# The sums of an attention group turned and inverted by one instruction each

## Chip, cores and metric

The kernel runs on one core of a Trainium2 chip. The metric is device time in microseconds (us) of one execution. Before the change three runs took 3507.87, 3508.98 and 3513.93 us, so the median is 3508.98.

## What is computed

One transformer block with adaptive layer norm: eight sequences of 1024 tokens, 512 features, 16 heads, everything in float32. A condition vector per sequence gives six modulation rows. They scale and shift two layer norms and gate the two residual additions, one of causal attention and one of an MLP with GELU.

```python
mod = jax.nn.silu(condition) @ Wada + bada
sh_a, sc_a, gt_a, sh_m, sc_m, gt_m = jnp.split(mod, 6, axis=1)
xm = layernorm(x, g1, be1) * (1.0 + sc_a[:, None, :]) + sh_a[:, None, :]
q, k, v = split_heads(xm @ Wqkv)                      # 16 heads of 32
scores = jnp.where(causal, q @ k.T * 32 ** -0.5, -jnp.inf)
attn = jax.nn.softmax(scores, axis=-1) @ v
x = x + gt_a[:, None, :] * (attn @ Wproj + bproj)
xm = layernorm(x, g2, be2) * (1.0 + sc_m[:, None, :]) + sh_m[:, None, :]
h = jax.nn.gelu(xm @ W1 + b1, approximate=False)
return x + gt_m[:, None, :] * (h @ W2 + b2)
```

## The kernel before

**Tiles and stages.** The tokens are cut into 16 blocks of 512 (`n` from 0 to 15; two for each sequence, an even one and an odd one, and the odd one also attends to the keys of the even one). The 16 heads of a block are cut into four groups of four (`g` from 0 to 3), because four heads of 32 features fill the 128 partitions. So there are 64 groups `(n, g)`.

**Attention of a group.** TensorE computes score tiles of four heads (`sc`, L1679) into `st`, one tile of four PSUM banks that scores and weights share. VectorE adds the causal mask on diagonal parts (L1691) and reduces each tile to row maxima (`mx`, L1694). In a few places scores are made one head at a time in the three other PSUM banks instead (`scores_by_heads`, L1649 and L1666), which is allowed when none of these is in use. The maxima are split into three bf16 parts (L1713 to L1716) and turned into a row by TensorE (L1732, copied by ScalarE at L1738). Then the scores are computed again transposed, with the maxima subtracted by a matmul (L1758, L1770), ScalarE takes the exponential (L1782) into one of three `pT` tiles, GpSimd clears what the mask excludes (L1787), TensorE multiplies by the values into `po` (L1810), and GpSimd adds the `pT` tiles of the group up (L1911).

**End of a group.** `finish` multiplies the added weights by a column of ones, which gives the softmax sums of four heads in a bank: 128 partitions by 512 tokens, where the 32 partitions of one head all hold the same 512 sums. ScalarE copies the bank to `rec` (L1840) and `po` to `top` (L1843). Only 4 x 512 of the 128 x 512 values are different, so not all are inverted. VectorE's transpose turns each 32 x 32 block on its own. After it, each column of a block is a copy of one column of 32 sums, so one column of each block is enough. `gather(i)` does this for a quarter of the tokens: it turns 128 columns of `rec` into the small tile `squares` (L1850) and inverts 4 of them (every 32nd) into `inverse` (L1852). `spread_out` turns `inverse`, read with each column repeated 32 times, back into `rec` (L1857), and `quotient` multiplies `top` by `rec` into `qT` (L1885, on GpSimd in most groups). `rec`, `top`, `squares` and `inverse` have one buffer each. For most groups the four `gather` and the `quotient` are put on a list of jobs. The group `first_end` and the last group do them at once, and the last group works on its four quarters one after the other.

**Linear work.** Between the attention instructions TensorE runs the projections, the MLP and the modulation (L217; L524 for the gates `a` and `m`), whose products go through the same three PSUM banks and are taken out by VectorE (L208, L194) or ScalarE (L197, L204). Weights come through a ring of eight buffers, loaded on SP's queue (L362, L364, L366). Early in the run sums of weight quarters are prepared for later use: `prep_up` and `prep_down` are loaded (L854), added on VectorE or GpSimd (L167, L170) and stored to DRAM as `kept_up_S` and `kept_down_S` (L823). Every DMA but a few is issued by SP, in order. Most blocks have their normalized rows turned by way of DRAM: `held_a` is stored (L713) and read back into `hat_a` (L718), and then scaled and shifted into `xm_a` (L775 on VectorE, L781 on ScalarE). The first two and the last two blocks have theirs turned by TensorE (L771).

**What sets the order.** The kernel writes each engine's order out by hand, with a planner. While it is being built, it keeps a clock for each engine (`now`) and a due time for each piece of data. Each `note(engine, ns, reads, writes)` moves these on by a planned cost. By them it decides at each step whether TensorE goes on with attention or with linear work (`step_aside`, `work`), whether a copy goes to VectorE or ScalarE (`sooner`), whether an addition goes to VectorE or GpSimd (`either`), and when a job is let in: `run_jobs` takes the next job once the planned VectorE clock and the job's data are not later than TensorE's.

```python
while jobs and (
    everything or (now["DVE"] <= now["PE"] and due(jobs[0][1]) <= now["PE"])
):
    jobs.pop(0)[0]()
```

The planned cost of a piece is 160 + 1.05 x 128 + 100 = 394 ns, that of a spread of 512 columns 140 + 1.05 x 512 = 678 ns. `norm_columns` (L486 to L496) runs twice, once for each layer norm; its intermediate `one_plus` has one buffer.

Of the kernel before, what the change touches and what calls it, by code (L numbers as in the profile page):

```python
# [9 lines left out]
F32 = mybir.dt.float32  # L10
# [12 lines left out]
def kernel(  # L23
# [33 lines left out]
    nc = tc.nc  # L57
    B, T, D = x.shape
    HD = W1.shape[1]
    P = 128  # L60
    hd = D // H
    scale = float(hd) ** -0.5
    TB = 512
    NTT = TB // P
    NHALF = T // TB
    NC = D // P
# [15 lines left out]
    small = ctx.enter_context(tc.tile_pool(name="small", bufs=2))  # L82
# [22 lines left out]
    def due(reads=(), writes=()):  # L105
        t = 0.0
        for k in reads:
            t = max(t, written.get(k, 0.0))
        for k in writes:
            t = max(t, left.get(k, 0.0))  # L110
        return t

    def note(engine, ns, reads=(), writes=(), port=False):
        start = max(now[engine], due(reads, writes))
        if port:
            start = max([start] + [b for a, b in pool_spans if a <= start < b])
        end = start + ns
        now[engine] = end
        if engine == "POOL":
            pool_spans.append((start, end))  # L120
            del pool_spans[:-16]
        for k in reads:
            left[k] = max(left.get(k, 0.0), end + SYNC)
        for k in writes:
            written[k] = end + SYNC
        return end
# [9 lines left out]
    def note_pe(ns, form, reads=(), writes=()):  # L136
        now["PE"] = max(now["PE"], due(reads, writes))
        if shape[0] != form:
            shape[0] = form
            now["PE"] += SWITCH  # L140
        note("PE", ns, reads)
        spent[0] += ns
        for k in writes:
            written[k] = now["PE"] + PIPE

    def note_act(ns, func, reads=(), writes=()):
        if func is not None and table[0] != func:
            table[0] = func
            ns += TABLE
        note("ACT", ns, reads, writes)  # L150
# [31 lines left out]
    def lin_bank():  # L182
        i = min(
            (i for i in range(3) if not live[i]),
            key=lambda i: left.get(("l", i), 0.0),
        )
        live[i] = True
        return i
# [54 lines left out]
    def mlp_steps(n):  # L243
        return [("u", n, i) for i in range(NQ)] + [("d", n, part) for part in range(4)]
# [9 lines left out]
    for w in range(1, NB):  # L254
        n = w - 1
        m = mlp_steps(n)
# [29 lines left out]
    n = NB - 1  # L286
# [115 lines left out]
    Q = P // NTT  # L402
# [81 lines left out]
    def spread(o):  # L484
        return cols[:, o : o + NC].unsqueeze(2).to_broadcast([P, NC, B])

    def norm_columns(name, shift_at, gain_at, o_g, o_b):

        gain = const.tile([P, NC, B], F32, tag=f"gain{name}", name=f"gain{name}")
        shift = const.tile([P, NC, B], F32, tag=f"shift{name}", name=f"shift{name}")  # L490
        one_plus = small.tile([P, NC, B], F32, tag="onep", name=f"onep{name}", bufs=1)
        nc.vector.tensor_scalar(one_plus, modT[:, ts(gain_at, NC), :], 1.0, None, ALU.add)
        nc.vector.tensor_tensor(gain, one_plus, spread(o_g), ALU.mult)
        nc.vector.tensor_tensor(shift, one_plus, spread(o_b), ALU.mult)
        nc.vector.tensor_tensor(shift, shift, modT[:, ts(shift_at, NC), :], ALU.add)
        return gain, shift  # L496
# [60 lines left out]
    def add_job(job, reads, first=False):  # L557

        at = sum(1 for other in jobs if other[2]) if first else len(jobs)
        jobs.insert(at, (job, reads, first))  # L560

    def run_jobs(everything=False):
# [4 lines that stand above are left out]
# [854 lines left out]
    def perform(step):  # L1421
        kind = step[0]
        if kind == "mod":
            yield from modulation(step[1])
        elif kind == "norm_columns_a":
            columns_of["a"] = norm_columns("a", 0, 1, O_G1, O_BE1)
        elif kind == "gates":
            yield from gates(step[1])
# [112 lines left out]
    def step_aside(reads, writes):  # L1541


        while threads():
            if linear_wait() == NEVER:
                hurry()
            own, other = wait_of((reads, writes)), linear_wait()
            if done_linear[0] < stream["due"]:
                if other > own + 100:
                    break  # L1550
            elif own <= max(other, 50):
                break
            work()
        while BANK in writes and bank_at() == NEVER:
            work()
        run_jobs()
        run_act_jobs()
        run_pool_jobs()
        run_preparation()
# [260 lines left out]
    def finish(n, g):  # L1820

        run_jobs(True)
        acc, slot = totals.pop((n, g))
        more = unadded if (n, g) == first_end else []
        step_aside([("acc", n, g), *(("p", slot) for *_, slot in more)], [BANK])
        bank = lin_bank()
        terms = [(0, TB, acc, slot)] + [(c0, w, pT, slot) for parts, pT, slot in more for _, c0, w, _ in parts]
        for i, (c0, w, term, held) in enumerate(terms):
            for j in range(HPG):
                r = slice(j * hd, (j + 1) * hd)  # L1830
                nc.tensor.matmul(  # L1831
                    banks[bank][r, TB - w :], ones, term[:, j, c0 : c0 + w],
                    start=i == 0, stop=i == len(terms) - 1, skip_group_check=True,
                )
            note_pe(2 * COLUMN * w, "columns", [("acc", n, g), ("p", held)], [("l", bank)])
        free_p.extend([slot, *(held for *_, held in more)])
        top = tmp.tile([P, TB], F32, tag="top", name=f"top_{n}_{g}", bufs=1)
        rec = tmp.tile([P, TB], F32, tag="rec", name=f"rec_{n}_{g}", bufs=1)
        kr = "rec"
        nc.scalar.copy(rec, banks[bank])  # L1840
        note_act(585, None, [("l", bank)], [kr])
        live[bank] = False
        nc.scalar.copy(top, outs.pop((n, g)))  # L1843
        note_act(585, None, ["po"], ["top"])
        part = TB // 4
        wide = TB // 4

        def gather(i):
            squares = small.tile([P, wide], F32, tag="squares", name=f"squares_{n}_{g}_{i}", bufs=1)
            nc.vector.transpose(squares, rec[:, ts(i, wide)])  # L1850
            some = inverse[:, ts(i, wide // Q)]
            nc.vector.reciprocal(some, squares.rearrange("p (a i) -> p a i", i=Q)[:, :, 0])  # L1852
            note("DVE", 160 + 1.05 * wide + 100, [kr], [kr])

        def spread_out(i=0, m=TB):
            some = inverse[:, i * m // Q : (i + 1) * m // Q].unsqueeze(2).to_broadcast([P, m // Q, Q])
            nc.vector.transpose(rec[:, ts(i, m)].rearrange("p (a i) -> p a i", i=Q), some)  # L1857
            note("DVE", 140 + 1.05 * m, [kr], [kr])

        inverse = small.tile([P, TB // Q], F32, tag="inverse", name=f"inverse_{n}_{g}", bufs=1)  # L1860
        if (n, g) == groups[-1]:
            for i in range(NTT):
                gather(i)
                spread_out(i, part)
                some = slice(i * part, (i + 1) * part)
                nc.vector.tensor_tensor(qTs[n][:, g, some], top[:, some], rec[:, some], ALU.mult)
                note("DVE", 200, [kr, "top"], [("att", n, i)])
            return

        if (n, g) == first_end:  # L1870
            for i in range(4):
                gather(i)
            spread_out()
            nc.vector.tensor_tensor(qTs[n][:, g, :], top, rec, ALU.mult)
            note("DVE", 700, [kr, "top"], [("att", n)], port=True)
            written["attended", n] = 0.0
            return

        def quotient():
            spread_out()  # L1880
            if n == NB - 1 and g == NC - 2:
                nc.vector.tensor_tensor(qTs[n][:, g, :], top, rec, ALU.mult)
                note("DVE", 700, [kr, "top"], [("att", n)], port=True)
            else:
                nc.gpsimd.tensor_tensor(qTs[n][:, g, :], top, rec, ALU.mult)  # L1885
                note("POOL", 1285, [kr, "top"], [("att", n)])
            if g == NC - 1:
                written["attended", n] = 0.0

        for i in range(4):  # L1890
            add_job(lambda i=i: gather(i), [kr], g == NC - 1)
        add_job(quotient, [kr], g == NC - 1)

    shared = {}
# [194 lines left out]
```

## Time and profile before

| | |
|---|---|
| median of three runs | 3508.98 us |
| the profiled execution, its own time | 3501.11 us |
| its span, first to last instruction | 3499.4 us |
| mean granted clock of TensorE | 0.998 |
| bytes moved by DMA | 498.84 MB, 143 GB/s on average |

The profile shows one execution. Busy time of an engine is the time in which it executes; register and semaphore instructions don't count. Groups of instructions are named by line, engine, operation and tiles (out<-in, with the shapes of both), and then come the count, the busy time in us, the mean ns of one, the idle time of the engine just before them, and what ended that idle time. A float32 matmul of the program shows as two records. A wait is named as engine, tile and line, "<-", what released it: total us, times, longest. A row of the timeline gives start and length in us, engine, line, operation, tiles and shapes, the number of instructions merged, and in brackets the idle time before with its releaser. The granted clock is a share of full speed.

### The profile page before, as it was taken

How to read it: one execution, taken by the hardware profiler on the slowest of the kernel's cores; microseconds unless marked ns; L12 is line 12 of the kernel's file. 1: busy time of each engine (PE TensorE's matmuls, PEld its weight loads, DVE VectorE, ACT ScalarE, POOL GpSimd, SP SyncE). 2: the span in 40 equal slices, each digit the busy share in tenths (PEclk: the TensorE clock that was granted, in tenths of full speed). 3: DMA queues.
4: the chain of work that ended last, by engine and by line, in shares of the span. 5: the costliest groups of instructions: out<-in, count | busy, mean ns of one | idle time of the engine just before them, and what ended most of it. 6: DMA issues, size and time to landing. Idle time of an engine off the chain costs nothing. (4 is left out here: it accounts for less than half of the span.)

```text
span 3499.4 us, 122173 instructions
## 1 busy us (share of the span) xinstructions
PE 3441.3 (98%) x55101; PEld 1750.9 (50%) x55101; DVE 2203.8 (63%) x2808; ACT 1212.8 (35%) x1272; POOL 2113.7 (60%) x2255
## 2 busy tenths in 40 slices
PE   8999999999999999999999999999999999999999
PEld 4444455445544555445554455544555445554555
DVE  5775675565666566565666656665666656656573
ACT  2335333342343513335232442333423333323521
POOL 3667847667366663767627676375762857628640
PEclk9999999999999999999999999999999999999999
DMA  6763444535535455363554535545455454543344
GB/s 213 237 188 104 137 125 139 147 104 171 147 118 158 119 162 149 103 182 116 152 152 127 159 116 152 153 137 146 130 154 143 130 144 132 154 126 98 104 134 140
DMA packets 335580, 498.84 MB, mean 143 GB/s; under 512 B 27724, under 2 KB 184460, under 8 KB 331476
## 3 DMA queue, kind: packets, MB, share of 16 engines
q1 hardware_dynamic: 334944, 490.99, 47.8%
q8 instruction: 434, 7.11, 0.8%
q14 instruction: 86, 0.70, 0.1%
q10 hardware_dynamic: 116, 0.03, 0.0%
HBM read 432.13 MB, written 56.69 MB: 140 GB/s over the span
## 5 line engine op out<-in xcount | busy, mean ns | idle before, releaser
L1911 POOL TENSOR_TENSOR pT<-pT,pT 128x256 f32<-128x256 f32 (+3 forms) x1254 | 1224.7, 1012 | 238.9 <-PE po L1810 123.9
L1782 ACT ACTIVATE pT<-st 128x2048 f32<-128x2048 f32 x288 | 541.1, 1879 | 1017.5 <-PE st L1770 886.3
L217 PE MATMUL bank<-w,hT 128*32 128x256 f32 x14336 | 822.1, 380 | 0.0
L1694 DVE TENSOR_REDUCE mx<-sc 128x4 f32<-128x2048 f32 (+3 forms) x383 | 663.3, 1753 | 200.5 <-PE sc L1679 194.7
L217 PEld LDWEIGHTS bank<-w,hT 128*32 128x32 f32 x14336 | 448.0, 110 | 389.8 <-issue 109.7
L217 PE MATMUL bank<-xm_m,w 128*32 128x256 f32 x8192 | 497.4, 381 | 2.3 <-ACT p_u L197 1.0
L217 PE MATMUL bank<-t_m,w 128*32 128x256 f32 x6144 | 384.0, 380 | 2.5 <-DVE qT L208 1.4
L217 PEld LDWEIGHTS bank<-xm_m,w 128*32 128x32 f32 x8192 | 255.5, 110 | 227.3 <-issue 56.6
L1787 POOL TENSOR_SCALAR_AFFINE_SELECT pT<-pT 128x512 f32<-128x512 f32 x256 | 177.3, 710 | 313.7 <-ACT pT L1782 313.3
L1679 PE MATMUL sc<-kT,qT 32*128 32x512 f32 (+3 forms) x3064 | 328.0, 520 | 3.1 <-DVE mx L1694 1.8
L1691 DVE TENSOR_TENSOR sc<-sc,mask 128x1024 f32<-128x1024 f32 (+1 forms) x160 | 162.8, 1017 | 255.2 <-PE sc L1679 210.8
L1810 PE MATMUL po<-pT,v 128*32 128x512 f32 (+3 forms) x3048 | 301.7, 490 | 2.5 <-POOL pT L1787 2.3
L1770 PE MATMUL st<-qT,kT 32*128 32x512 f32 (+3 forms) x3072 | 302.7, 487 | 0.0
L217 PEld LDWEIGHTS bank<-t_m,w 128*32 128x32 f32 x6144 | 188.9, 110 | 178.8 <-issue 49.8
L217 PE MATMUL bank<-xm_a,w 128*32 128x256 f32 x3968 | 241.6, 380 | 2.4 <-ACT p_k L197 1.1
L1679 PEld LDWEIGHTS sc<-kT,qT 32*128 32x128 f32 x3064 | 129.2, 183 | 182.4 <-issue 82.4
L208 DVE TENSOR_TENSOR hT<-bank,u_u 128x512 f32<-128x512 f32 x186 | 126.0, 686 | 127.2 <-PE bank L217 126.5
L217 PE MATMUL bank<-t_a,w 128*32 128x256 f32 x2944 | 182.3, 380 | 1.4 <-ACT qT L204 0.9
L1885 POOL TENSOR_TENSOR qT<-top,rec 128x512 f32<-128x512 f32 x61 | 79.8, 1309 | 170.7 <-DVE rec L1857 167.8
L217 PE MATMUL bank<-w,qT 128*32 128x512 f32 (+1 forms) x1824 | 175.4, 515 | 3.7 <-DMA w<-in_L_cond_Wproj_dram 3.7
L1199 ACT ACTIVATE hT<-hT,cols 128x512 f32<-128x512 f32 x256 | 164.7, 711 | 40.7 <-DVE hT L208 27.4
L217 PEld LDWEIGHTS bank<-xm_a,w 128*32 128x32 f32 x3968 | 123.9, 110 | 101.3 <-issue 16.9
(262 smaller groups left out, 3657.1 us busy)
## 6 DMA issues: line engine op xcount, KB each, us to landing
w<-in_L_cond_W_dram SPq DMA_DIRECT2D x384, 256.0 KB
w<-kept_up_S SPq DMA_DIRECT2D x256, 256.0 KB
w<-kept_down_S SPq DMA_DIRECT2D x256, 256.0 KB
w<-kept_qkv_S SPq DMA_DIRECT2D x180, 256.0 KB
w<-in_L_cond_Wqkv_dram SPq DMA_DIRECT2D x147, 256.0 KB
hat_a<-in_x_dram SPq DMA_DIRECT2D x64, 256.0 KB
xr<-in_x_dram SPq DMA_DIRECT2D x32, 512.0 KB
out_dram<-xr SPq DMA_DIRECT2D x31, 512.0 KB
```

What stands on the lines that cost most here:

```text
L208: nc.vector.tensor_tensor(out, src, other, op)
L217: nc.tensor.matmul(ps[r, :], columns, rhs, start=start, stop=stop, skip_group_check=True)
L1199: nc.scalar.activation(hT[:, i, :], hT[:, i, :], AF.Gelu, bias=cols[:, O_B1 + f : O_B1 + f + 1])
L1679: nc.tensor.matmul(sc[:, j, c0 : c0 + w], qTs[n][r, gg, ts(qt, P)], keys_of(n, kh)[r, gg, :w], start=True, stop=True, skip_group_check=True,)
L1691: nc.vector.tensor_tensor(place, place, shape_of.to_broadcast(place.shape), ALU.add)
L1694: nc.vector.tensor_reduce(maxima[n, gg][:, kh, qt, :], sc[:, :, c0 : c0 + w], axis=AX.X, op=ALU.max)
L1770: nc.tensor.matmul(st[:, j, c0 : c0 + w], kT[r, gg, ts(k % NTT, P)], qT[r, gg, TB - w :], start=False, stop=True, skip_group_check=True,)
L1782: nc.scalar.activation(pT[:, :, :used], st[:, :, :used], AF.Exp, scale=scale)
L1787: nc.gpsimd.affine_select(diagonal, diagonal, pattern=[[0, HPG], [1, P]], compare_op=ALU.is_ge, fill=0.0, base=0, channel_multiplier=-1,)
L1810: nc.tensor.matmul(po[r, TB - w :], v[:, k % NTT, g * P + j * hd : g * P + (j + 1) * hd], pT[:, j, c0 : c0 + w], start=(k == 0), stop=last ...
L1885: nc.gpsimd.tensor_tensor(qTs[n][:, g, :], top, rec, ALU.mult)
L1911: nc.gpsimd.tensor_tensor(into, into, pT[:, j, c0 : c0 + w], ALU.add)
```

## The change

`gather` no longer uses `squares`. It turns a whole stretch of `rec` in place, 512 columns for most groups, and inverts every 32nd column of it, 16 in one instruction. So a group has one job for it where it had four. The last group still goes by quarters of 128 columns, in place too. The planned costs are written anew: 325 + 1.27 x 512 = 975 ns for the whole gather, where the four pieces had 4 x 394 = 1578 ns, and 180 + 1.04 x 512 = 712 ns for the spread. `one_plus` gets two buffers, its pool's default. Lines behind L1846 move up by two to four: the turn is at L1848, the reciprocal at L1850, the spread at L1855 and the product at L1882.

```diff
-        one_plus = small.tile([P, NC, B], F32, tag="onep", name=f"onep{name}", bufs=1)
+        one_plus = small.tile([P, NC, B], F32, tag="onep", name=f"onep{name}")
...
-        wide = TB // 4
-
-        def gather(i):
-            squares = small.tile([P, wide], F32, tag="squares", name=f"squares_{n}_{g}_{i}", bufs=1)
-            nc.vector.transpose(squares, rec[:, ts(i, wide)])
-            some = inverse[:, ts(i, wide // Q)]
-            nc.vector.reciprocal(some, squares.rearrange("p (a i) -> p a i", i=Q)[:, :, 0])
-            note("DVE", 160 + 1.05 * wide + 100, [kr], [kr])
+
+        def gather(i, m=TB):
+            nc.vector.transpose(rec[:, ts(i, m)], rec[:, ts(i, m)])
+            some = inverse[:, i * m // Q : (i + 1) * m // Q]
+            nc.vector.reciprocal(some, rec[:, ts(i, m)].rearrange("p (a i) -> p a i", i=Q)[:, :, 0])
+            note("DVE", 325 + 1.27 * m, [kr], [kr])
 
         def spread_out(i=0, m=TB):
...
-            note("DVE", 140 + 1.05 * m, [kr], [kr])
+            note("DVE", 180 + 1.04 * m, [kr], [kr])
...
         if (n, g) == groups[-1]:
             for i in range(NTT):
-                gather(i)
+                gather(i, part)
                 spread_out(i, part)
...
         if (n, g) == first_end:
-            for i in range(4):
-                gather(i)
+            gather(0)
             spread_out()
...
-        for i in range(4):
-            add_job(lambda i=i: gather(i), [kr], g == NC - 1)
+        add_job(lambda: gather(0), [kr], g == NC - 1)
         add_job(quotient, [kr], g == NC - 1)
```

## The prediction

> **What bounds the kernel now.** I read the busy times first, then the run cut into stages, then TensorE's waits by stage, then the groups that the diff touches.
>
> ```profile
> span 3499.4 us, 122173 instructions
> PE 3441.3 (98%) x55101; PEld 1750.9 (50%) x55101; DVE 2203.8 (63%) x2808; ACT 1212.8 (35%) x1272; POOL 2113.7 (60%) x2255
> 0.00:118.00 118.00, 102.07 (x1877) 59.18 (x1877) 75.65 (x113) 32.94 (x40) 52.66 (x74) 1.00 0.69 221
> 118.00:477.00 359.00, 348.50 (x5304) 168.02 (x5304) 248.81 (x318) 130.13 (x127) 262.34 (x290) 0.99 0.51 156
> 477.00:3300.00 2823.00, 2798.86 (x44716) 1417.89 (x44708) 1772.95 (x2231) 996.14 (x1043) 1729.95 (x1834) 1.00 0.48 138
> 3300.00:3499.40 199.40, 191.88 (x3221) 105.78 (x3212) 106.36 (x147) 53.63 (x64) 68.74 (x59) 0.99 0.44 131
> ```
>
> In a stage row stand its bounds, its length, the busy time of PE, PEld, DVE, ACT and POOL, the granted clock, DMA's share and GB/s. PE is busy for 3441.3 of 3499.4 us, so all waits together are 58.1 us: 15.9 in the first stage, 10.5 in the second, 24.1 in the third, 7.5 in the last. The matmuls are the same before and after, so a gain can only come out of these waits (and out of stretches at a lower clock). VectorE, which the change relieves, is idle for 37% of the span.
>
> I cut at 118 and 477 us because of the change's second effect. The kernel records its instructions in an order that it plans with the costs in `note`. I compared both programs' orders on TensorE, counting four column-tile matmuls as one step: the first 425 steps are the same; then, up to the weights of block 2, group 2 (`st_2_2_2`, the 44th exponential, at 478.96 us here), only 1477 of 1726 stand in the same sequence; of the 9994 after that, 9901 do, from block 3 to the end. So the change is a reordering in the second stage and nearly nothing but shorter DVE work in the third.
>
> **The gather.** The last number before the second bar is the mean ns of one instruction; in the row of L686 stand minimum, median and maximum; in the two timeline rows start and length in us.
>
> ```profile
> L1850 DVE STREAM_TRANSPOSE squares<-rec 128x128 f32<-128x128 f32 x256 | 78.6, 307 | 60.0 <-ACT rec L1840 54.6
> L1852 DVE RECIPROCAL inverse<-squares 128x4 f32<-128x4 f32 x256 | 45.7, 178 | 8.8
> L1857 DVE STREAM_TRANSPOSE rec<-inverse 128x512 f32<-128x512 f32 x63 | 44.6, 708 | 2.9
> L704 DVE STREAM_TRANSPOSE xm_a<-hat_a 128x512 f32<-128x512 f32 x56 | 34.9, 674 | 0.0
> L686 DVE RECIPROCAL rstd_m<-rstd_m x4: 128/129/164, 3387.9 to 3393.9; 128x1 f32<-128x1 f32 x4
> 1313.10 0.30 DVE L1850 STREAM_TRANSPOSE squares<-rec 128x128 f32<-128x128 f32 x1
> ...
> 1315.33 0.71 DVE L1857 STREAM_TRANSPOSE rec<-inverse 128x512 f32<-128x512 f32 x1
> ```
>
> Removed per group: 4 x (307 + 178) = 1.94 us busy, 2.23 us on the clock (1313.10 to 1315.33). Added: one turn of 512 columns in place. No row shows one. The lower bound is 674 (L704), the upper 4 x 307 = 1228, as if nothing were saved; I take 700, near L704 and L1857, which have its shape. Then one reciprocal of 16 columns: at least 178, at most 178 + 12 x (178 - 129)/3 = 374 by the step from one column to four; I take the middle, 276. The gather is then 0.98 us (0.85 to 1.60), 0.96 us of busy time less (0.34 to 1.09), for 63 of 64 groups 60 us of DVE. The last group keeps its four pieces of 128 columns, in place: the same eight instructions, nothing saved.
>
> [...]
>
> The spread, L1857, is unchanged but for its planned cost. The second buffer of `one_plus` removes a wait between two uses that lie over 100 us apart: nothing. The price of a longer single instruction is that a PSUM copy behind it waits up to 0.98 us and not 0.31. In the old order the four pieces already stand back to back in 39 of 64 groups, so I take nothing, with 2 us as the upper bound (25 other groups, of which one in six would meet a PE wait by 0.5 us). New planned costs also swap some copies and normalizations between DVE and ACT (each under ten, of like duration): nothing; ACT's 65% idle time covers them.
>
> **Third stage.** These are the larger rows in which TensorE waited for DVE there:
>
> ```profile
> PE bank L1732 <- DVE mcols L1716: 1.5, 2, 0.9
> PE bank L217 <- DVE qT L208: 1.4, 2, 1.0
> PE st L1758 <- DVE mx L1694: 1.2, 3, 0.8
> PE bank L1732 <- DVE y L208: 1.1, 1, 1.1
> PE sc L1679 <- DVE mx L1694: 0.9, 2, 0.7
> PE bank L217 <- DVE t_m L793: 0.9, 2, 0.6
> ```
>
> Together 7.0 us, the most that a quicker DVE can give back; below, nothing. A gather is in front of the awaited instruction only now and then, so I take a sixth: -1.2 us.
>
> **Second stage.** What the new order puts side by side is costed with these rows (mask, reductions, exponential, turn; then TensorE's own pieces):
>
> ```profile
> L1691 DVE TENSOR_TENSOR sc<-sc,mask 128x1024 f32<-128x1024 f32 x96 | 118.2, 1231 | 150.9 <-PE sc L1679 109.6 <-issue 19.8 <-ACT top L1843 13.2
> L1694 DVE TENSOR_REDUCE mx<-sc 128x4 f32<-128x1536 f32 x64 | 112.5, 1757 | 2.2
> L1694 DVE TENSOR_REDUCE mx<-sc 128x4 f32<-128x512 f32 x64 | 43.5, 680 | 0.0
> L1694 DVE TENSOR_REDUCE mx<-sc 128x4 f32<-128x2048 f32 x191 | 437.3, 2290 | 197.2 <-PE sc L1679 194.7
> L1666 DVE TENSOR_REDUCE mx<-bank 128x1 f32<-128x512 f32 x4 | 2.6, 678 | 1.0 <-PE bank L1649 1.0
> L1782 ACT ACTIVATE pT<-st 128x2048 f32<-128x2048 f32 x288 | 541.1, 1879 | 1017.5 <-PE st L1770 886.3
> L771 PE MATMUL bank<-ident,hat_m 128*128 128x128 f32 x64 | 11.3, 303 | 3.3 <-ACT hat_m L691 3.3
> 142.38 1.14 PE L1679 MATMUL sc<-kT,qT 32*128 32x512 f32 x8 [0.84 <-ACT pT L1782]
> 143.35 1.03 PE L1649 MATMUL bank<-kT,qT 32*128 32x512 f32 x6
> 146.57 1.21 PE L1649 MATMUL bank<-kT,qT 32*128 32x512 f32 x1 [2.19 <-DVE mx L1666]
> 161.03 1.05 PE L1810 MATMUL po<-pT,v 128*32 128x384 f32 x16
> ```
>
> The scores by heads (L1649) stood behind one score tile and cost 0.84 + 2.19 = 3.03 us. Now they go first, and a score tile and the next weights, which share the one `st` tile, follow with nothing between: DVE has four head reductions and one of a tile, 4 x 0.678 + 2.29 = 5.00 us, TensorE has three heads and the tile, 1.03 + 1.14 = 2.17; the wait is 2.83, or -0.2. Later the diagonal scores of group (2,3) (384 and 128 columns) are followed at once by weights, covered by one turn of `hat_m` (two records of 0.30): 1.231 + 1.757 + 0.680 - 0.60 = +3.1. And after `st_2_0_2` only one pair of `po` matmuls covers the exponential: 1.88 - 1.05 = +0.8. Against that stand the other old waits of this stage, 10.5 - 3.0 = 7.5 us, which the new order may keep or drop; since the other neighbours on the `st` tile stand about as far apart as before, I let a third go: -2.5. Sum +1.2, with bounds of -7.7 and +3.7 before DMA and clock.
>
> DMA: SP issues in order, and the new order moves four stores of `kept_down` and four loads of `prep_down`, 256 KB each, from behind to ahead of `hat_a` of block 2 and the weights after it (`w_57`).
>
> ```profile
> 112.00:152.00 40.00, 34.45 (x618) 17.70 (x611) 29.30 (x52) 11.94 (x11) 26.24 (x38) 0.93 1.02 320
> 137.55 2.08 SPq L718 DMA_DIRECT2D hat_a<-held_a  x4
> 150.68 1.00 DVE L775 TENSOR_SCALAR xm_a<-hat_a,gaina,shifta 128x512 f32<-128x512 f32 x2 [1.31 <-DMA b_out_m<-in_L_cond_b_dram]
> 160.57 0.64 PE L217 MATMUL bank<-xm_a,w 128*32 128x256 f32 x8
> 144.00:148.00 4.00, 1.80 (x14) 0.90 (x12) 3.71 (x4) 0.00 (x0) 4.00 (x7) 0.82 1.09 218
> 148.00:152.00 4.00, 4.00 (x20) 1.15 (x13) 1.97 (x4) 1.11 (x1) 1.21 (x2) 0.50 1.04 311
> 152.00:156.00 4.00, 4.00 (x21) 1.36 (x20) 1.79 (x3) 2.17 (x3) 1.66 (x2) 0.83 0.50 157
> ```
>
> The DMA engines are full there (1.02), so 8 x 0.262 MB at 320 GB/s come 6.6 us later. TensorE first needs `xm_a` 9.9 us after DVE starts on it; that cover hides the delay, and I take 0, with +6.6 as the upper bound (the delay uncovered). The same loads then leave the lighter time after 156 us, which can only help.
>
> The clock: after the 3.03 us of waits it read 0.82, 0.50 and 0.83 in three slices of 4 us, a loss of 4 x (0.18 + 0.50 + 0.17) = 3.4 us. The changed order waits about as long there, and once more for 3.1 us; I take 0, the bounds are -3.4 and +3.4. [...]
>
> **Sum**: 0 (first stage) + 1.2 + (-1.2) + 0 (last) = 0.0. The profiled execution took 3501.1 us; the median of the runs is 3509.0, 7.9 above it. I predict 3509.
>
> **Rivals.** *Faster.* The waits are not a third but wholly gone and the clock holds: -7.7 - 3.4 in the second stage, and -1.2: -12.3, 3497; half of it would not count. For it: DVE gets 60 us, and planned costs closer to the rows (394 planned for a piece against 485). Against it: the new order has more short covers, not fewer.
>
> *Slower.* `hat_a` comes 6.6 us late. DVE executes in order, so the reductions and the gathers behind L775 stand too, the `st` tile is not released, and TensorE stands before the cover of 9.9 us is of use. Price: 6.6, and the second low-clock stretch, 3.4: +10.0, 3519. It decides once DVE's wait at L775 exceeds about 4 us, where it is 1.31 now. For it: the share of 1.02, and two of the gate weights (L524) now load behind `hat_a`. Against it: in the new order too, the scores by heads, the rest of group (0,3) and half of the gate matmuls stand between, and need none of these.
>
> *It doesn't do what it says*: the turn in place costs 1228 and the reciprocal 374, and DVE saves only 0.34 us a group. Third stage -0.4: 3510, inside no change.
>
> **How the numbers follow.** Forecast 0.50, the turn that saves little 0.04, faster 0.20, slower 0.26. About 0.2% (7 us) is what a measurement here can tell from no change; so faster 0.20, within 0.54, slower 0.26. The range goes from 3498, nearly the whole faster case, to 3523, the slower one with the +3.7 bound; the forecast's own range is 3503 to 3515.
>
> **What would show it.** Right: the turn at L1848 near 0.70 us and the reciprocal at L1850 near 0.28; DVE busy near 2144; waits of about 10 us between the same two landmarks, and 22 to 24 in the third stage; an `st` wait of some 3 us after the scores of group (2,3). Wrong: DVE waiting over 4 us for `hat_a` at L775; a second stretch of clock under 0.9 before 500 us; or third-stage waits that differ by more than 4 us, which would mean that an order that is almost the same runs differently.

## The result and the profile after

The changed kernel took 3525.86 us (median of six runs, 3521.07 to 3527.74), the kernel before on the same chip 3507.64 us (six runs, 3500.90 to 3513.93). The ratio is 1.0058, with a 95% interval from 1.0048 to 1.0069: slower by 18 us by the medians, outside the range that was predicted. The profiled execution of the changed kernel took 3527.74 us, the longest of its six, and that of the kernel before 3501.11, near its shortest. So what is read from the two profiles adds up to 26.6 us, some 8 more than the medians differ.

First the busy times on the profile's page, then the stages (bounds, length, busy time of PE, PEld, DVE, ACT and POOL, granted clock, DMA's share, GB/s), cut at the same landmarks as before: the 44th exponential now starts at 500.86 us and not at 478.96.

```profile
span 3526.0 us, 121791 instructions
PE 3450.0 (98%) x55101; PEld 1754.9 (50%) x55101; DVE 2147.4 (61%) x2428; ACT 1214.7 (34%) x1278; POOL 2110.1 (60%) x2252
0.00:118.00 118.00, 101.13 (x1865) 58.75 (x1868) 74.29 (x108) 33.03 (x40) 51.80 (x72) 1.00 0.68 218
118.00:501.00 383.00, 358.52 (x5352) 171.86 (x5349) 246.93 (x268) 131.39 (x130) 260.04 (x289) 0.97 0.48 148
501.00:3326.00 2825.00, 2797.98 (x44690) 1418.04 (x44686) 1721.02 (x1913) 997.38 (x1046) 1729.03 (x1834) 1.00 0.47 138
3326.00:3526.00 200.00, 192.36 (x3208) 106.21 (x3200) 105.19 (x141) 52.92 (x64) 69.21 (x59) 0.98 0.42 131
```

TensorE's waits are 16.9, 24.5, 27.0 and 7.6 us in the four stages (length less PE busy), where they were 15.9, 10.5, 24.1 and 7.5. The second stage is 24 us longer: 14.0 us more waiting, and 10.0 us more PE busy time. Its granted clock is 0.97, where it was 0.99; read in slices of 4 us from 100 to 504 us, the clock lost 11.9 us (sum of 4 x (1 - clock)), where it lost 3.4.

The groups of the gather, by shape (line, engine, operation, tiles, count, busy us, mean ns, idle before):

```profile
L1848 DVE STREAM_TRANSPOSE rec<-rec 128x512 f32<-128x512 f32 x63 | 44.0, 699 | 50.9 <-ACT rec L1840 50.9
L1850 DVE RECIPROCAL inverse<-rec 128x16 f32<-128x16 f32 x63 | 16.0, 253 | 2.2
L1855 DVE STREAM_TRANSPOSE rec<-inverse 128x512 f32<-128x512 f32 x63 | 44.6, 708 | 1.4
```

The instructions do what was forecast: 0.95 us busy for a gather where the four pieces took 1.94, and VectorE is 56 us less busy. The loss is not in them.

To place it I compared the starts of the same exponential in the two timelines. The changed kernel is late by 0.9 us at the first one, 3.6 at number 13, 1.2 at 25 (315.92 us in the old run), 11.3 at 31, 20.4 at 37, 22.2 at 43 (475.04 us), and 25.3 at 283 of 288. A single start can also move because attention and linear work are interleaved otherwise, but the slices say the same: of the 22.5 us by which waits and lost clock grew in and just ahead of this stage, 15.9 lie between 340 and 504 us (10.8 of waits and 5.1 of clock). TensorE's waits from 340 to 504 us, before and after (total us, times, longest):

```profile
PE st L1758 <- DVE mx L1694: 2.1, 2, 1.6
PE bank L1732 <- POOL mcols L1716: 1.3, 1, 1.3
```

```profile
PE bank L217 <- ACT p_v L197: 2.9, 1, 2.9
PE bank L771 <- ACT hat_m L664: 2.9, 1, 2.9
PE bank L1732 <- POOL mcols L1716: 2.5, 1, 2.5
PE bank L217 <- DVE t_m L1097: 2.5, 1, 2.5
PE st L1758 <- DVE mx L1694: 2.3, 3, 1.5
PE sc L1679 <- ACT pT L1782: 1.0, 1, 1.0
```

Three waits became eight, and four of the new ones are 2.5 to 2.9 us each, for four different producers. None is the gather. What they have in common is that the producer, or what it needs, stands in order on a queue behind other work. The clearest is the wait for `p_v`, followed back here in the timeline of after (start, length, instruction, idle time before it):

```profile
366.26 1.89 DVE L704 STREAM_TRANSPOSE xm_a<-hat_a 128x512 f32<-128x512 f32 x3
375.69 0.70 DVE L1691 TENSOR_TENSOR sc<-sc,mask 128x512 f32<-128x512 f32 x1 [7.54 <-PE sc L1679]
385.31 0.70 DVE L704 STREAM_TRANSPOSE xm_a<-hat_a 128x512 f32<-128x512 f32 x1
398.37 2.93 ACT L781 ACTIVATE xm_a<-hat_a,shifta,gaina 128x512 f32<-128x512 f32 x4 [9.53 <-DMA hat_a<-held_a]
405.12 0.58 ACT L197 COPY p_v<-bank 128x512 f32<-128x512 f32 x1 [3.35 <-POOL y_d L170]
405.76 3.97 PE L217 MATMUL bank<-w,xm_a 128*32 128x256 f32 x40 [2.88 <-ACT p_v L197]
```

Of the four turns of block 3's normalized rows, three stand at 366.26 us. The fourth is recorded later, behind a mask that waits 7.54 us for its scores, and executes at 385.31. The rows go to DRAM and back only when all four are turned, so ScalarE starts on `xm_a` 11.4 us later than in the old order; its copy into `y_d`, GpSimd's addition to that and `p_v` follow. In the old order the four turns stood together:

```profile
368.52 2.48 DVE L704 STREAM_TRANSPOSE xm_a<-hat_a 128x512 f32<-128x512 f32 x4
...
386.93 1.51 ACT L781 ACTIVATE xm_a<-hat_a,shifta,gaina 128x512 f32<-128x512 f32 x2
```

### The profile page after: what moved, and what is told of

Its sections match the earlier page's. It is cut to its first block, busy times and chain, and to the rows that moved or that the text cites. A ratio compares the mean times of both kernels' runs of the same rounds, so it can differ in the third digit from the quotient of the medians.

```text
span 3526.0 us, 121791 instructions
## 1 busy us (share of the span) xinstructions
PE 3450.0 (98%) x55101; PEld 1754.9 (50%) x55101; DVE 2147.4 (61%) x2428; ACT 1214.7 (34%) x1278; POOL 2110.1 (60%) x2252
## 5 line engine op out<-in xcount | busy, mean ns | idle before, releaser
L1882 POOL TENSOR_TENSOR qT<-top,rec 128x512 f32<-128x512 f32 x61 | 79.3, 1300 | 181.6 <-DVE rec L1855 140.0
```

## Experiments

Ratios are to the kernel before, run beside each kernel on the same chip, with 95% intervals. Its own median was 3503.4 to 3507.6 us in these series.

**Instruction or order.** The change does two things, new instructions and a new order (by new planned costs and one job for four). Each was run alone. In the first, the new instructions stand where the fourth piece stood, and the plan is the old one:

```diff
+        def planned():
+            note("DVE", 160 + 1.05 * part + 100, [kr], [kr])
+        def quarter_job(i):
+            if i == 3:
+                gather(0)
+            planned()
...
-        add_job(lambda: gather(0), [kr], g == NC - 1)
+        for i in range(4):
+            add_job(lambda i=i: quarter_job(i), [kr], g == NC - 1)
```

> The new instructions (one turn of 512 columns in place, one reciprocal of 16, for 63 groups) at the place of the fourth piece, with the planned costs and the four jobs of before, so that every other instruction of all five queues stands in the order of before. Theory ORDER (the time is lost by the new order of the second stage, not by the instructions): 3500 to 3509 us, ratio to before 0.998 to 1.001, VectorE's busy time near 2145 us, and waits in the stage from 118 us to the 44th exponential near 10 us. Rival INSTRUCTION (one long job in place holds VectorE, or makes a copy late, when it counts): 3518 us or more, ratio over 1.003.

Measured: 3503.89 us, ratio 0.9992 (0.9983 to 1.0000), with 12.0 us of waits in the second stage of its profile. In the second, the four old pieces run as one job, planned with the new costs, so that every queue has the changed kernel's order:

```diff
+        def gather(i, m=TB):
+            for at in range(i * m // part, (i + 1) * m // part):
...
+            note("DVE", 325 + 1.27 * m, [kr], [kr])
...
-        for i in range(4):
-            add_job(lambda i=i: gather(i), [kr], g == NC - 1)
+        add_job(lambda: gather(0), [kr], g == NC - 1)
```

> The old four pieces with the small tile, issued together by one job with the new planned costs, so that every other instruction stands in the order of after. Theory ORDER: 3521 to 3532 us, ratio 1.004 to 1.007, with 28 us or more of waits between 118 us and the 44th exponential, as after has them. Rival INSTRUCTION: 3505 to 3513 us, since the costly instruction is gone.

Measured: 3530.86 us, ratio 1.0070 (1.0056 to 1.0084), with 26.7 us of waits in the second stage (the changed kernel has 24.5, not the 28 of the expectation). So the order carries the whole loss, and the instructions, with the second buffer of `one_plus`, gain 0.08% in the old order (0 to 0.17%). The waits of the two show the same from 340 to 504 us: 5.9 us of waits in the first (`st` 4.6, `mcols` 1.3), and in the second the changed kernel's list, with the old instructions:

```profile
PE bank L771 <- ACT hat_m L664: 3.0, 1, 3.0
...
PE bank L217 <- ACT p_v L197: 2.8, 1, 2.8
PE bank L1732 <- POOL mcols L1716: 2.5, 1, 2.5
PE bank L217 <- DVE t_m L1097: 2.5, 1, 2.5
```

**One job or new costs.** Both parts of the planning edit, one at a time; each gives an order of its own. First, the changed kernel's single job with the old costs:

```diff
-            note("DVE", 325 + 1.27 * m, [kr], [kr])
+            note("DVE", (160 + 1.05 * part + 100) * m / part, [kr], [kr])
...
-            note("DVE", 180 + 1.04 * m, [kr], [kr])
+            note("DVE", 140 + 1.05 * m, [kr], [kr])
```

> After, but planned with the old sums: 4 x 394 = 1578 ns for the gather and 678 ns for the spread, in one job. This gives a third order of the second stage, the same as neither before nor after. Theory ORDER: any time from 3503 to 3530 us, and the difference from before lies between 118 us and the 44th exponential again; if it is near 3507, the planned costs did it, if near 3525, the one job for four did. Rival INSTRUCTION: 3520 to 3530 us whatever the order.

Measured: 3510.11 us, 1.0011 (1.0001 to 1.0020). Then the old kernel's four jobs with the new costs:

```diff
-            note("DVE", 160 + 1.05 * wide + 100, [kr], [kr])
+            note("DVE", (325 + 1.27 * TB) / 4, [kr], [kr])
...
-            note("DVE", 140 + 1.05 * m, [kr], [kr])
+            note("DVE", 180 + 1.04 * m, [kr], [kr])
```

> Before (four pieces, four jobs, the small tile), planned with the new sums: 975 / 4 = 244 ns for a piece and 712 ns for the spread. A fourth order of the second stage. Theory ORDER: any time from 3503 to 3530 us; near 3525 the planned costs alone do it, near 3507 they don't. Rival INSTRUCTION: 3505 to 3511 us, since all instructions are the old ones.

Measured: 3516.21 us, 1.0024 (1.0014 to 1.0034). Neither part alone makes the whole loss: the single job gives 0.1%, the new costs 0.24%, and only both together gave this order.

**Which stage.** The new instructions everywhere, and `new_plan` chooses the plan by block: the new costs and one job where it is true, the old costs and four jobs elsewhere. With `new_plan = n < 2` the order is the changed kernel's up to the 44th exponential and the old one behind it:

> The new instructions everywhere; planned with the new costs and as one job for blocks 0 and 1, with the old costs and as four jobs for blocks 2 and 3. Up to the 44th exponential the order is the changed kernel's, after it the order of before. Theory SECOND STAGE (all of the loss arises up to about 500 us): 44th exponential at 498 to 503 us, time 3519 to 3527. Rival LATE ORDER (a part of the loss comes from the last tenth of a per cent of the order, from block 3 to the end): 3508 to 3516.

Measured: 3517.55 us, 1.0038 (1.0023 to 1.0052), between the ranges of the two theories, and the 44th exponential 18 us late. The 340 to 504 us slice is as in the changed kernel (14.6 us of waits, 5.1 lost to the clock; there 14.1 and 5.1). The reverse, `new_plan = n > 0`:

> The reverse: planned with the old costs and as four jobs for block 0, the new ones for blocks 1 to 3; 1713 of 1726 steps of the second stage as before, the late order as in the changed kernel. Theory SECOND STAGE: 3503 to 3511, the 44th exponential at 478 to 482 us. Rival LATE ORDER: 3512 to 3520.

Measured: 3501.94 us, 0.9989 (0.9980 to 0.9999). With the old early order the late one costs nothing, so the loss hangs on the order of the second stage. The first of the two is 0.2% under the changed kernel with intervals that just overlap. In the profiled executions the second stage waits as long in both (24.3 and 24.5 us), and the third 19.0 and 27.0 us, where the kernel with the same late order and the old early one has 23.4. What makes that difference isn't settled. With `new_plan = n == 0`, block 0 alone:

> The new instructions everywhere; only block 0 planned with the new costs and as one job. 1658 of 1725 early steps stand as in the changed kernel, with block 3's four turns split as there; the late order is that of before. Theory SPLIT TURN and theory SECOND STAGE: 3517 to 3527. If the 67 steps that differ hold a large part of the loss: 3508 to 3516.

Measured: 3517.08 us, 1.0035 (1.0025 to 1.0046): the plan of the first block alone draws an order with 0.35 of the 0.58%.

**Which pieces.** The changed kernel, of which single pieces are moved, while planned costs and all else stay. First the split turn:

```diff
-            into = by_tile[:, :, :, t, :]
+            for at in ([2, 3] if t == 2 else []) if key == "a3" and t > 1 else [t]:
+                into = by_tile[:, :, :, at, :]
...
```

> The changed kernel, in which one VectorE instruction moves: the fourth turn of block 3's hat_a is recorded with the third (all other instructions on all five queues in the changed kernel's order). Theory SPLIT TURN (most of the loss is the fourth turn, 19 us behind the third, in order behind a mask that waits 7.5 us for its scores; held_a, hat_a and xm_a follow it 11 to 15 us late): ACT's first xm_a of block 3 starts near 387 us and not 398, the 44th exponential near 482 to 488 us, time 3508 to 3516. Rival WHOLE ORDER (the split turn is one of several lost covers, TensorE's waits between 340 and 504 us have other chains): the 44th exponential at 494 to 501, time 3520 to 3527. If only PE's waits at 405.8 us go (2.9 us, with the low clock after them about 5): 3519 to 3522.

Measured: 3520.31 us, 1.0039 (1.0025 to 1.0053), with the 44th exponential at 495.32. That is in the ranges of the rival, WHOLE ORDER, and also what was expected if only TensorE's wait at 405.8 us went. The interval overlaps that of the changed kernel, so the gain is not clear of noise. The wait it was aimed at did shrink, by the chain that was read: with the four turns together `xm_a` starts 6.6 us earlier (the edit moves later lines by one), and the wait for `p_v` is 1.0 where it was 2.9.

```profile
362.32 2.48 DVE L705 STREAM_TRANSPOSE xm_a<-hat_a 128x512 f32<-128x512 f32 x4
...
391.81 2.93 ACT L782 ACTIVATE xm_a<-hat_a,shifta,gaina 128x512 f32<-128x512 f32 x4 [7.03 <-DMA hat_a<-held_a]
```

```profile
PE bank L217 <- ACT p_v L197: 1.0, 1, 1.0
```

The other three waits have a GpSimd instruction in their chain. In the changed kernel's timeline the maxima of group (1,3) stand behind two additions to `hT`, the quotient of (1,3), which `t_m` needs, behind eight additions to `pT`, and `hat_m` behind a copy to `rec` that waits for the quotient of (2,0):

```profile
359.24 4.69 POOL L170 TENSOR_TENSOR hT<-hT,hT 128x1024 f32<-128x1024 f32 x2
363.88 1.25 POOL L1713 CAST mcols<-mx 128x16 bf16<-128x16 f32 x1
...
446.22 5.96 POOL L1907 TENSOR_TENSOR pT<-pT,pT 128x384 f32<-128x384 f32 x8
452.14 1.26 POOL L1882 TENSOR_TENSOR qT<-top,rec 128x512 f32<-128x512 f32 x1
...
491.86 0.58 ACT L1840 COPY rec<-bank 128x512 f32<-128x512 f32 x1 [5.39 <-POOL qT L1882]
...
492.82 2.23 ACT L664 ACTIVATE hat_m<-xr,offset_m,rstd_m 128x512 f32<-128x512 f32 x3
```

So three pieces went to VectorE, at the same place of the program:

```diff
-        engine = nc.gpsimd if on_pool else nc.vector
+        engine = nc.gpsimd if on_pool and (n, g) != (1, 3) else nc.vector
...
+                engine = nc.vector if (n, g) in [(1, 3), (2, 0)] else nc.gpsimd
+                engine.tensor_tensor(qTs[n][:, g, :], top, rec, ALU.mult)
```

> The changed kernel, in which three pieces that stood on GpSimd behind additions to hT and pT run on VectorE at the same place of the program: the split of the maxima of group (1,3) (four instructions), the quotients of groups (1,3) and (2,0). Planned costs and all else as in the changed kernel. Theory POOL QUEUE (TensorE's waits for mcols at 366.9 us, 2.5; for t_m at 454.6, 2.5; for hat_m at 493.7, 2.9; each with a stretch of low clock behind it): these waits fall to under 1 us each, 44th exponential at 488 to 495 us, time 3513 to 3520. Rival (the waits only move to the next late producer, VectorE being late too): time 3522 to 3528. In the second case the three rows are there again with another releaser.

Measured: 3515.91 us, 1.0034 (1.0021 to 1.0046), a time as the first theory had it, but its rows say that only one of the three waits went:

```profile
PE st L1758 <- DVE mx L1694: 4.1, 2, 2.5
PE bank L1732 <- DVE mcols L1716: 3.6, 2, 3.2
...
PE bank L771 <- ACT hat_m L664: 1.2, 1, 1.2
```

The wait for `t_m` is gone. That for `hat_m` is 1.2 (it was 2.9), but the wait on `st` right behind it, at 486.21 us, grew from 0.6 to 2.5: with `hat_m` in time, the mask and the reductions of group (2,3) decide, and the two waits together are 3.7 us where they were 3.5. The wait for `mcols` only got a new releaser and grew from 2.5 to 3.2, since two of VectorE's pieces took 2.25 us each and ended with GpSimd's additions (rows in the last section). With the turns together as well:

> The same three pieces on VectorE, and the fourth turn of block 3 with the third. Theory OFF-PATH QUEUES (the loss between 320 and 500 us is made of such single late pieces, which add up): 44th exponential at 480 to 488 us, time 3505 to 3514. Rival (the order as a whole, in which attention lags the linear work, leaves TensorE without cover whatever single piece is mended): time 3515 to 3524.

Measured: 3514.93 us, 1.0032 (1.0021 to 1.0044), at the lower edge of the rival's range, with the 44th exponential at 494.77 where the theory had 480 to 488. What single pieces give back does not add up. The next one leaves the split on GpSimd and records the two additions behind it:

```diff
+            if hold[0]:
+                later.append((out, a, b, op))
+            else:
+                nc.gpsimd.tensor_tensor(out, a, b, op)
...
+        if (n, g) == (1, 3):
+            while later:
+                nc.gpsimd.tensor_tensor(*later.pop(0))
```

> The changed kernel with the two late quotients on VectorE and the turns together as before, but the split of the maxima of group (1,3) stays on GpSimd and is recorded ahead of two additions to hT that stood in front of it. Theory OFF-PATH QUEUES (the split on VectorE only got a new releaser, 3.2 us, beside a busy GpSimd; in front of GpSimd's additions it is early): the wait for mcols near 367 us is gone, time 3505 to 3512. Rival (the order's lost cover, TensorE then stands for the next piece of block 1): 3513 to 3519, with TensorE's idle time from 340 to 504 us again 10 to 12 us.

Measured: 3515.76 us, 1.0023 (1.0014 to 1.0031). TensorE no longer waits for `mcols`, and from 340 to 504 us the list begins (lines moved by the edit):

```profile
PE st L1768 <- DVE mx L1701: 4.3, 3, 2.5
PE bank L221 <- ACT p_v L201: 3.1, 1, 3.1
PE po L1820 <- POOL pT L1797: 1.9, 1, 1.9
```

By the ratios, mending four late pieces takes back some 0.35 of 0.58%. But the waits in this slice are still 11.9 us, as the rival expected: the additions that were moved back make `pT` late (1.9), and `p_v` is late again. In this order TensorE comes close to what is being made at the time, and when one piece is early it stands for the next. Where the rest of the loss lies, piece by piece, was not taken further.

**Chance or cause.** Is a gather planned as one short job a bad plan as such? The same kernel with the one planned number changed, to the measured 952 ns (`302 + 1.27 * m`) and to 1075 ns (`425 + 1.27 * m`), where the change has 975:

> The changed kernel with one number of the plan changed: the gather is planned with 952 ns (as measured: 699 + 253) where it was 975; one job as in the change. 1505 of 1725 steps of the second stage stand as in the changed kernel. Theory CHANCE (small changes of the plan draw another order, whose quality has nothing to do with how true the costs are): any time from 3500 to 3530, the loss against before again in the first 500 us. Rival SYSTEMATIC (a gather planned as one short job makes orders that are worse): 3518 to 3530.

Measured: 3504.18 us, 1.0007 (0.9997 to 1.0016).

> The same with a planned gather of 1075 ns, 100 above the change's, 123 above the measured one; 1439 of 1725 steps of the second stage as in the changed kernel. Theory CHANCE: any time from 3500 to 3530, and not the same as with 952 ns. Rival SYSTEMATIC: 3514 to 3530, and nearer to before than with 952, since the plan is nearer to the old 1578.

Measured: 3500.99 us, 0.9995 (0.9986 to 1.0004). A planned cost that differs by 23 ns, the truer one, takes the loss away within the noise, and one that is wrong by 123 ns does as well. The two times are not clearly different from each other. The systematic theory falls: the planner's order is a draw, and the change drew a bad one. The waits from 340 to 504 us are 4.3 and 4.7 us in these two.

**A version that is faster than both.** The kernel with the old plan for block 0 and the new one elsewhere was run once more:

> The kernel that planned block 0 with the old costs as four jobs and all else with the new ones, once more: if it is faster than before, the ratio is 0.998 to 0.9995 again and its interval stays under 1; if the first result was the end of a spread, 0.9995 to 1.0005.

Measured: 3502.68 us, 0.9987 (0.9978 to 0.9996). Together with 0.9989 before, it is faster than the old kernel by about 0.1%, some 4 us. That is near the 0.9992 of the new instructions in the old order; whether the few steps that differ add anything is not shown.

## Why the prediction was wrong

**The gather: right.** Turn 0.699 us (forecast 0.700), reciprocal 0.253 (0.276), VectorE busy 2147.4 us (2144). A column of the reciprocal beyond the fourth cost (253 - 178)/12 = 6.3 ns; the rows had led to bounds of 0 and 16. The middle that the forecast took, 8.2, was too high. With the old order the ratio was 0.9992 (0.9983 to 1.0000), which agrees with -1.2 us and a forecast of no change for this part.

**First, third and last stage: right within what one execution can tell.** The third stage's waits are 27.0 us (22 to 24 forecast, 24.1 before), 2.9 more; the kernel with the old early order and the new late one has 23.4 and 22.3 in its two profiles, and was not slower. That an order which is almost the same runs alike held.

**Second stage: the step that failed is "of the other old waits, 7.5 us, the new order lets a third go".** The places where I named a pair on the `st` tile came out near the forecast. After the scores of group (2,3), 3.1 us were forecast:

```profile
493.70 0.33 PE L771 MATMUL bank<-ident,hat_m 128*128 128x128 f32 x1 [2.85 <-ACT hat_m L664]
494.66 0.61 PE L1758 MATMUL st<-mrow,minus_ones 32*128 32x384 bf16 x8 [0.63 <-DVE mx L1694]
```

That is 3.48 us, though most of it with another releaser: the turn of `hat_m`, which I counted as cover, was late itself. Behind `st_2_0_2` it was 0.8 forecast and 1.00 measured. At the scores by heads, -0.2 was forecast: the new wait on `st` came as worked out (2.38, forecast 2.83), but the old one of 2.16 stayed beside it, so 4.5 us in place of the 2.8 that the sum left there. With these three taken out, 15.5 of the 24.5 us remain, where the sum had 5.0. This 10.5 is most of the error, and four waits of the new order make it up: 2.9 for `p_v`, 2.7 on `po`, 2.5 for `mcols` and 2.5 for `t_m` (the one on `po` belongs to the term for DMA, which the sum put at 0). I weighed the new order only by the neighbours on TensorE that share `st`, and assumed that all else would wait as before or less. The reordering also moved pieces on VectorE, GpSimd and ScalarE, and these were what TensorE came to wait for: the split turn, the maxima and the quotients behind additions, `hat_m` behind the quotient, and the copy of `po` behind a late `hat_a` (below). That could have been looked for in the order of those queues, which is known before a run; how long each wait would be could not.

**The clock: forecast 0, bounds of 3.4, measured 8.5 us.** The slices of 4 us behind the new waits (2.5 us at 366.85, 2.9 at 405.76) show the granted clock, third number from the right:

```profile
368.00:372.00 4.00, 4.00 (x52) 1.99 (x48) 0.15 (x1) 0.73 (x1) 4.00 (x5) 0.57 0.19 66
404.00:408.00 4.00, 2.24 (x24) 1.10 (x28) 0.69 (x1) 2.37 (x2) 3.84 (x4) 0.71 0.26 64
408.00:412.00 4.00, 4.00 (x52) 1.49 (x48) 0.00 (x0) 1.53 (x2) 4.00 (x4) 0.87 0.36 110
```

The stretches lose 4 x 0.43 and 4 x (0.29 + 0.13), that is 1.7 us each time; behind the 2.9 at 493.70, two slices of 0.80 and 0.77 lose 1.7 again. The rows of before already showed 3.4 us lost after 3.03 us of waits, but the sum held a new wait of 3.1 us and put its clock at nothing without a reason. The rest is missing because the waits behind it were: the 8.5 us are five stretches of 1.7. One of them follows a wait of 2.3 us for a weight at 117.84, just ahead of this stage, which the other kernel with the same early order doesn't show. Over the whole run the two profiled executions differ by 26.6 us, of which 17.9 are waits and 8.7 PE busy time.

**DMA and the slower rival: its condition came true, its price did not.** `hat_a` of block 2 was issued at 146.34 us (137.55 before), and VectorE waited at L775 for 6.0 us, over the 4 us from which the rival decides. But the reductions behind L775 were not what TensorE needed next, and it didn't wait for `xm_a` either. It was hit by way of ScalarE:

```profile
158.72 2.22 ACT L781 ACTIVATE xm_a<-hat_a,shifta,gaina 128x512 f32<-128x512 f32 x3 [2.76 <-DMA hat_a<-held_a]
160.85 0.56 ACT L1840 COPY rec<-bank 128x512 f32<-128x512 f32 x1
161.31 0.57 ACT L1843 COPY top<-po 128x512 f32<-128x512 f32 x1
...
161.99 1.55 PE L1810 MATMUL po<-pT,v 128*32 128x512 f32 x16 [2.71 <-issue]
```

ScalarE waits for `hat_a`, the copy of `po` to `top` stands behind it, and TensorE starts on `po` 0.11 us after that copy ends (the view names no releaser; that it is this copy is inferred from the times). The price is 2.7 us of wait and one stretch of clock (0.91 and 0.66 in the slices from 160 to 168 us, 1.7 us): 4.4 where the rival had 10.0. In the kernel with the same early order and the old late one, this wait was 0.4 us, but the one at the scores by heads 3.95 where the changed kernel had 2.16. So the size of a single wait is that of one execution.

So by the profiles the forecast of no change failed by 14.0 - 1.2 = 12.8 us of waits and 8.5 us of clock in and just ahead of the second stage. The chance of slower, 0.26, was too low for a reason that stood in the prediction's own numbers: 249 of 1726 steps were out of sequence, each move can make or cover a wait, and the old order, with 10.5 us of waits in 359, had more to lose than to win. The other orders with the new instructions bear this out: with 1.0035, 1.0011, 1.0007, 0.9995 and 0.9989, none is clearly faster than the same instructions in the old order (0.9992). How bad the draw was is chance all the same: with the plan of 952 ns the forecast would have come out right, at 3504 us, and by luck, since no step of its sum tells these orders apart.

## What to carry over

In a kernel whose order comes from a planner, a change of a planned cost is a redraw of the order, and by these runs the orders of the same instructions spread from 0.9987 to 1.0058, several times the 0.1% that the better instruction gave; run an edit once with the old order kept, so that its own worth is seen, and choose the order by measurement. When a new order is judged before it runs, follow the off-path queues as well: for each piece that TensorE needs, see what now stands ahead of its producer in order on VectorE, ScalarE, GpSimd and the DMA queue, above all pieces of one set that are no longer together. And where TensorE's cover is thin, mending one wait uncovers the next, so the gain of several repairs is not their sum.

## What the runs showed of the hardware

**Behind eight of 13 waits of 2.2 to 2.9 us the granted clock read less than 1.00.** In the changed kernel's profile 1.7 us were lost after each of the waits of 2.3 us (at 117.84), 2.7, 2.5, 2.9 and 2.9, and 3.4 after one of 2.35 (at 3420.25) and after the pair of 2.16 and 2.38 (at 147.26 and 151.62). The waits of 2.6 us at 17.45, 2.3 at 31.89 and at 3011.28, 2.5 at 454.58 and 2.2 at 646.28 were followed by 1.00 throughout. Behind one of 3.2 at 364.57 in the kernel with three pieces on VectorE the 16 score matmuls at 366.43 took 1.03 us; in the changed kernel the same 16 took 1.92 (at 369.19) behind the wait of 2.5. So the length alone doesn't decide; what does is not shown.

**Two small VectorE instructions were long beside GpSimd's additions, and ended with them.** With the split of the maxima on VectorE, a cast of 128 x 16 took 2.25 us, and ended when GpSimd's addition did (356.27 + 4.69 = 360.96, and 358.77 + 2.25 = 361.02; the next one at 363.30, GpSimd's at 363.26). In the changed kernel a cast of the same size took 0.20 us on VectorE while GpSimd stood idle (at 419.43):

```profile
356.27 4.69 POOL L170 TENSOR_TENSOR hT<-hT,hT 128x1024 f32<-128x1024 f32 x2
360.91 2.35 POOL L170 TENSOR_TENSOR hT<-hT 128x1024 f32<-128x1024 f32 x1
```

```profile
358.77 2.25 DVE L1713 CAST mcols<-mx 128x16 bf16<-128x16 f32 x1
361.05 2.25 DVE L1714 TENSOR_TENSOR rest<-mx,mcols 128x16 f32<-128x16 f32 x1
```

Why they end together is not shown. The piece that moved from a busy GpSimd to VectorE was not done sooner after its maxima: 5.8 us behind them, and 5.1 on GpSimd in the changed kernel.

**A transpose in place took about as long as one into another tile** (699 ns at 512 columns, beside 674 into another tile and 708 from a repeated input), and a reciprocal of 16 columns took 253 ns where one of four columns took 178.
